# A list schedule of a four-layer graph network on one core: new offsets, new margins, one buffer moved from one pool to another

## The chip, the cores and the metric

The kernel runs on one core of a Trainium2 chip. The metric is the device time in microseconds of one execution; lower is better. All arithmetic is in fp32.

## The reference

There are 128 graphs of 64 nodes with 512 features each, so 8192 rows of 512. Four layers follow each other, and every layer ends in a residual and a layer norm:

```python
x = _layernorm(x + L0(x, adj))       # (A @ x) @ w, A from s = (x @ w) @ a by tanh, leaky relu, exp, row sums
x = _layernorm(x + L1(x, adj))       # q, k, v; weight = adj * exp(q k^T) / row sum; weight @ v
x = _layernorm(x + L2(x, adj, mask)) # w = (q . (adj @ k)) / sqrt(512); softmax over the nodes, times v = x @ Wv
x = _layernorm(x + L3(x, adj))       # hypergraph conv 512 -> 1024, relu, layer norm, conv 1024 -> 512, + x
```

In L3 the conv is `D^-1 H B^-1 H^T (x @ W^T) + b` with `H = (adj != 0)`.

## The kernel before

**Tiling.** A tile is 128 rows, two graphs. A group is two tiles (`GT = 2`, 256 rows), and there are `NG = 32` groups. Two groups make a pair (`SG = 2`) for the first product of L3. Adjacency is loaded and prepared for chunks of four tiles, so for two groups at a time.

**Products.** A product with a weight matrix is cut into blocks of half its size and done with seven block products instead of eight (`seven_products`); the first product of L3, with w3a, applies this twice and does 49 products for a pair of groups (`forty_nine_products`). The combined weight blocks are computed once, stored in DRAM, and streamed again for every group through a pool of 4 KB-per-partition buffers named `ring` (`streamed`). The matrices m1 and m2, the products of the q and k weights of L1 and L2, stay resident. Activations, transposes and sums of blocks live in a pool named `k4`, of buffers of the same size. `bank` is PSUM, eight banks. `product` and `inner` are counters without memory: they limit how many series of seven block products may be under way.

**Modes of TensorE.** Most matmuls use the whole 128x128 array ("whole"). Gathers over a graph, scores and value products use parts of it ("quarters", "columns"); the text calls these divided. One operation of a gather or of scores has 16 or 8 matmuls; fp32 makes two instructions of each.

**Order.** The body of the kernel doesn't emit instructions. It adds operations to an `Order` object: engine, planned cost, buffers read and written, and a key. `run(g)` and `run_rest` give a group's operations the step 0 to 15 they belong to; `keys_by_what_follows` then sets an operation's step to `BASE[group]` plus a part of 16 by how long a chain hangs on it, so `BASE` says how far apart groups are planned. The key is that step less an urgency and less `EARLY[step]` (and `LEAD` for the first group of a pair). `PREPARED` gives the keys of the preparation of weights, beside the groups. A piece of a streamed weight after the first is drawn towards the first one by the share `TOGETHER`.

`Order.run` then simulates the engines at build time. It has planned costs (`w_pe`, `w_dve`, `w_act`, `w_pool`), delays from one engine to the next (`LATENCY`, `AGAIN`, `TO_PE`), and a link for loads with `BYTES_PER_NS` and at most `UNDERWAY` transfers. At each moment every free engine takes the ready operation of the lowest key whose buffers are free. `AHEAD` stops the loads (engine SP) at so many steps past the oldest unfinished operation. For TensorE, `choose` decides between whole and divided operations: from the whole mode it goes to a divided one if its key is lower than that of the first whole one by more than `NEAR`, or by more than 0 when at least `ENOUGH` divided matmuls are ready; in a divided mode it stays as long as a divided operation within `FAR` of the first whole one is ready. `TURN` and `TURN_DIVIDED` are the planned costs of a change of mode. `BLOCK` and `REST` keep divided matmuls apart in time. Finally the operations are emitted in the order found, and each engine's instructions are pinned to that order (line 1472 emits them all, so every instruction has this line). All loads and stores are issued on SP's queue.

Of the kernel before, what the change touches and what calls it, by code (L numbers as in the profile page):

```python
# [28 lines left out]
APART = 4  # L29

BASE = [
    0.0, 1.743, 3.111, 5.372, 10.971, 14.755, 18.98, 22.38, 27.28, 30.68, 35.58, 38.98, 43.88, 47.28, 52.18, 55.58,
    60.48, 63.88, 68.78, 72.18, 77.08, 80.48, 85.38, 88.78, 93.68, 97.08, 101.98, 105.38, 110.213, 112.471, 117.658, 118.432,
]
RESIDENT = ("m1", "m2")
APART_3A = (0, NG // SG - 1)
LEAD = [2.505, -0.294]
PREPARED = [-3.906, 7.537, 8.271, 13.522, 12.862, -0.62]
PIECE = 1024
EPS = 1e-5  # L40
TINY = 1.1754944e-38
# [24 lines left out]


class Order:
    LATENCY = {"PE": 210, "DVE": 125, "ACT": 140, "POOL": 120, "SP": 2200}
    AGAIN = {"PE": 0, "DVE": 115, "ACT": 115, "POOL": 120}  # L70
    TO_PE = 300
    BYTES_PER_NS = 300
    UNDERWAY = 8
    TURN, TURN_DIVIDED = 145, 60

    NEAR = 0.5
    FAR = 6.79728
    ENOUGH = 28.88843999999999

    EARLY = [2.22, 0.626, 0.0, -0.759, 0.0, -0.394, 0.0, 1.328, 0.0, 1.09, 0.384, -0.03, -0.766, -0.36, -1.408, -0.964]  # L80

    BLOCK = 64
    REST = 4500
    AHEAD = 4.2
    TOGETHER = 0.7

    def __init__(self, slots):
        self.slots = {kind: list(range(n))[::-1] for kind, n in slots.items()}
# [74 lines left out]
    def run(self):  # L163

        ready = {e: [] for e in self.LATENCY}
        free_at = {e: 0 for e in self.LATENCY}
        number = {o: i for i, o in enumerate(self.ops)}
        events, n, link, mode, began = [], 0, 0, None, [-self.REST] * self.BLOCK
        port_free, port_user, landed = 0, None, []
        for o in self.ops:  # L170
            if not o.missing:
                heappush(ready[o.engine], (o.key, number[o], o))
        by_step, front = sorted((o for o in self.ops if o.engine != "SP"), key=lambda o: o.step), 0
        done, now = [], 0
        while len(done) < len(self.ops):
            moved = False
            while front < len(by_step) and by_step[front].start is not None:
                front += 1
            far = by_step[front].step + self.AHEAD if front < len(by_step) else float("inf")
            for e, heap in ready.items():  # L180
                while free_at[e] <= now:
                    skipped, held, found, found_pe = [], set(), None, {}
                    while heap:
                        if e == "SP" and heap[0][0] > far:
                            break
                        item = heappop(heap)
                        need = defaultdict(int)
                        wants = [b for b in item[2].touches if b.slot is None]
                        for b in wants:
                            need[b.kind] += 1  # L190
                        if item[2].port and port_free > now:
                            skipped.append(item)
                        elif all(k not in held and len(self.slots[k]) >= c for k, c in need.items()):
                            if e == "PE":
                                skipped.append(item)
                                found_pe.setdefault(item[2].mode, []).append((item, wants))
                                if item[0] < 0:
                                    break
                            else:
                                found, takes = item, wants  # L200
                                break
                        else:
                            held.update(k for k, c in need.items() if k in held or len(self.slots[k]) < c)
                            skipped.append(item)
                    if found_pe:
                        chosen = self.choose(found_pe, mode, now, began)
                        if chosen is None:
                            n += 1
                            heappush(events, (now + 100, n, None, None))
                        else:  # L210
                            found, takes = chosen
                            skipped.remove(found)
                    for item in skipped:
                        heappush(heap, item)
                    if found is None:
                        break
                    moved, found = True, found[2]
                    turn = 0
                    if e == "PE":
                        if found.mode == "any":  # L220
                            found.mode = "whole" if mode in ("whole", None) else "quarters"
                            found.args = (found.mode == "whole",)
                        if found.mode != mode:
                            turn = self.TURN if "whole" in (found.mode, mode) else self.TURN_DIVIDED
                        mode = found.mode
                        began += [now + turn + found.cost * i // found.matmuls for i in range(found.matmuls)]
                    found.start = now
                    done.append(found)
                    found.takes = takes
                    for b in takes:  # L230
                        b.slot = self.slots[b.kind].pop()
                    end = free_at[e] = now + found.cost + turn
                    if found.port:
                        port_free = end
                        if e == "POOL":
                            found.behind = port_user
                        else:
                            port_user = found
                    if e == "SP":
                        link = max(link, now) + found.bytes // self.BYTES_PER_NS  # L240
                        end = max(end, link)
                        landed.append(end + self.LATENCY[e])
                        if len(landed) >= self.UNDERWAY:
                            free_at[e] = max(free_at[e], landed[-self.UNDERWAY])
                    seen = end + self.LATENCY[e]
                    heappush(events, (free_at[e], n, None, None))
                    for u in found.users:
                        n += 1
                        heappush(events, (seen if e == "SP" else end + self.AGAIN[e] if u.engine == e
                                          else seen + self.TO_PE * (u.engine == "PE"), n, u, None))  # L250
                    for b in found.touches:
                        n += 1
                        heappush(events, (seen, n, None, b))
                    n += 1
            if not events:
                stuck = [(e, h[0][2].key, [b.kind for b in h[0][2].touches]) for e, h in ready.items() if h]
                raise RuntimeError(f"no operation can start: {len(done)} of {len(self.ops)}, {stuck}")
            now = max(now, events[0][0])
            while events and events[0][0] <= now:
                _, _, u, b = heappop(events)  # L260
                if u is not None:
                    u.missing -= 1
                    if not u.missing:
                        heappush(ready[u.engine], (u.key, number[u], u))
                if b is not None:
                    b.left -= 1
                    if not b.left:
                        self.slots[b.kind].append(b.slot)
        return done
# [19 lines left out]
def kernel(  # L289
# [32 lines left out]
    kinds = {}  # L322

    def kind(name, n, *shape, space=None):
        kinds[name] = [(space or sbuf).tile([P, *shape], FP, name=f"{name}{i}") for i in range(n)]

    kind("x", 6, GT, D)
    kind("k4", 18, PIECE)
    kind("ring", 8, PIECE)
    kind("h", 2, GT, DH)  # L330
    kind("k2", 2, D)
    kind("adj", 6, CT, N)
# [2 lines left out]
    kind("e", 4, GT, N)  # L335
    kind("col", 28, 16)
    kind("bank", 8, D, space=psum)
    kinds["product"] = [None] * 2
    kinds["inner"] = [None] * 3

    order = Order({k: len(v) for k, v in kinds.items()})
# [332 lines left out]
    for h in range(2):  # L674
        load_half(wq2_raw, wqk_h[0], h)
        load_half(wk2_raw, wqk_h[1], h)
    order.key = PREPARED[0]
    m2 = gram("m2", wq2_raw, wk2_raw, KC // 2)
# [668 lines left out]
    def run_rest(n):  # L1347
# [65 lines left out]
        for r, (g, xt, _, in_g, own, dc, dh) in enumerate(pair):  # L1413
            step(13)
            order.early += LEAD[0] * (n - 1 - r)
            h, sh = hs[r], Buf("col", GT)
# [7 lines left out]
            step(14)  # L1424
            order.early += LEAD[1] * (n - 1 - r)

# [116 lines left out]
```

## Time and profile before

| | |
|---|---|
| median of 3 runs | 2156.91 us (2156.62 to 2159.59) |
| profiled execution, its own time | 2155.14 us |
| its span, first to last instruction | 2153.2 us |
| PE busy | 2120.1 us, 98% of the span |
| DVE, ACT, POOL busy | 1403.6, 1204.8, 460.0 us |
| moved by DMA | 422.34 MB, mean 196 GB/s |
| DMA issues of 512 KB ring<-3a | 196, median 4.5 us to landing |

All instructions stand under line 1472, so groups are told apart by what they write and read: `bank<-ring,k` is a product of a streamed weight with an activation, `bank<-k,m` one with a resident matrix, `bank<-kept,h`, `bank<-e,x` and `bank<-kept,x` are gathers, `bank<-k,k` of 64 columns is scores, `bank<-k,e` the value product, `bank<-ident,x` a transpose. PE is the stream of matmuls and PEld that of weight loads. A busy PE is not PE at its peak, since ends of matmuls are modelled; starts are measured.

### The profile page before, as it was taken

To read this page: it belongs to the slowest core of one execution; us is meant where nothing else is said; L and a number is where in the kernel's file an instruction comes from. 1 tells how busy PE (TensorE), PEld (TensorE's weight loads), DVE (VectorE), ACT (ScalarE), POOL (GpSimd) and SP (SyncE) were. 2 spreads that over 40 slices of the span, in tenths; PEclk is the share of its full clock that TensorE was granted. 3 is DMA by queue.
4 is the path that set the end of the run, shared out by engine and by line. 5 is a ranking of instruction groups with operands and counts; after the bars stand their busy time and mean duration, and the time that the engine had idled before them with its cause. 6 is when DMAs were issued, how large, how long until landed. Compare 5 with 4: busy or idle time off the path is not lost.

```text
span 2153.2 us, 53735 instructions
## 1 busy us (share of the span) xinstructions
PE 2120.1 (98%) x21419; PEld 1829.5 (85%) x21419; DVE 1403.6 (65%) x4150; ACT 1204.8 (56%) x2698; POOL 460.0 (21%) x434
## 2 busy tenths in 40 slices
PE   8999999999999999999999999999999999999997
PEld 4897788888888888888888888888888888888875
DVE  5756767575666758567576766757667585676644
ACT  2544755565655746466464664646557464674554
POOL 1211422122212122131211211122121221302221
PEclk9999999999999999999999999999999999999999
DMA  8888784554546545474554655545465454555455
GB/s 275 276 294 292 263 284 153 207 182 149 194 164 218 188 153 197 148 241 171 181 183 141 214 175 189 199 153 189 161 221 181 159 194 145 207 185 171 170 187 190
DMA packets 166313, 422.34 MB, mean 196 GB/s; under 512 B 34928, under 2 KB 52528, under 8 KB 166064
## 3 DMA queue, kind: packets, MB, share of 16 engines
q1 hardware_dynamic: 166064, 418.92, 56.9%
q8 instruction: 169, 2.77, 0.5%
q14 instruction: 80, 0.66, 0.1%
HBM read 382.77 MB, written 36.08 MB: 195 GB/s over the span
## 4 chain that ended last, share of the span: by engine, by line
PE 92%; DMA 4%; SPq 1%; ACT 1%; DVE 1%; issue 0%; POOLq 0%; ACTq 0%; DVEq 0%
PE bank L1472 92%; DMA ring<-3a 3%; SPq L1472 1%; ACT k L1472 1%; DMA adj<-in_adjT_dram 0%; DMA k<-in_wk_dram 0%; ACT h L1472 0%; DMA x<-in_x_dram 0%; DMA 3a<-k 0%; DMA ring<-in_wv_dram 0%; DMA adj<-mask_rows 0%; DVE h L1472 0%; DVE col L1472 0%; DVE x L1472 0%; DVE k L1472 0%
## 5 line engine op out<-in xcount | busy, mean ns | idle before, releaser
L1472 PE MATMUL bank<-ring,k 128*128 128x256 f32 x4940 | 1191.1, 388 | 16.0 <-DMA ring<-3a 8.6
L1472 PEld LDWEIGHTS bank<-ring,k 128*128 128x128 f32 x4940 | 901.6, 190 | 170.5 <-issue 34.1
L1472 ACT COPY k<-bank 128x256 f32<-128x256 f32 (+1 forms) x934 | 428.0, 483 | 437.7 <-PE bank L1472 426.8
L1472 DVE SCALAR_TENSOR_TENSOR x<-bank,col,x 128x256 f32<-128x256 f32 (+1 forms) x736 | 367.6, 504 | 301.3 <-PE bank L1472 291.6
L1472 PEld LDWEIGHTS bank<-k,m 128*128 128x128 f32 x3584 | 432.5, 192 | 13.3 <-ACT k L1472 1.9
L1472 PE MATMUL bank<-k,m 128*128 128x128 f32 x3584 | 442.2, 276 | 0.5 <-ACT k L1472 0.5
L1472 DVE TENSOR_TENSOR k<-bank,k 128x256 f32<-128x256 f32 x582 | 235.6, 420 | 193.3 <-PE bank L1472 127.4
L1472 POOL TENSOR_TENSOR col<-col,mhalf 128x2 f32<-128x2 f32 (+1 forms) x161 | 113.8, 707 | 1025.1 <-DVE col L1472 631.7
L1472 ACT ACTIVATE k<-x,col 128x512 f32<-128x512 f32 x256 | 184.2, 720 | 199.3 <-DVE col L1472 186.5
L1472 PE MATMUL bank<-ring,h 128*128 128x256 f32 x1024 | 236.1, 379 | 0.0
L1472 ACT ACTIVATE x<-x,col,col 128x512 f32<-128x512 f32 x256 | 197.2, 812 | 45.5 <-DVE col L1472 45.2
L1472 PEld LDWEIGHTS bank<-ring,h 128*128 128x128 f32 x1024 | 189.8, 190 | 24.5
L1472 DVE TENSOR_TENSOR k<-k 128x256 f32<-128x256 f32 (+1 forms) x349 | 155.9, 468 | 23.4 <-ACT k L1472 20.8
L1472 DVE TENSOR_TENSOR k<-k,k 128x256 f32<-128x256 f32 (+3 forms) x361 | 165.1, 465 | 0.8
L1472 POOL TENSOR_TENSOR k<-k,b3b_b 128x512 f32<-128x512 f32 x64 | 81.6, 1286 | 196.9 <-ACT k L1472 160.3
L1472 PEld LDWEIGHTS bank<-k,k 128*64 128x64 f32 (+1 forms) x2112 | 79.4, 140 | 43.3 <-issue 31.8
L1472 PE MATMUL bank<-k,k 128*64 128x64 f32 (+1 forms) x2112 | 110.0, 239 | 4.6 <-DMA k<-in_wk_dram 4.5
L1472 DVE TENSOR_SCALAR col<-col 128x2 f32<-128x2 f32 (+2 forms) x402 | 84.0, 214 | 33.1 <-ACT k L1472 23.4
L1472 ACT ACTIVATE k<-bank,u_c 128x128 f32<-128x128 f32 x256 | 84.8, 364 | 31.9 <-PE bank L1472 31.7
L1472 POOL TENSOR_TENSOR k<-k,k 128x1024 f32<-128x1024 f32 (+1 forms) x31 | 72.0, 2324 | 128.2 <-DVE k L1472 69.7
L1472 POOL TENSOR_TENSOR x<-x,bv_b 128x512 f32<-128x512 f32 x64 | 82.3, 1291 | 62.1 <-PE bank L1472 36.9
L1472 DVE TENSOR_TENSOR h<-k,k 128x1024 f32<-128x1024 f32 (+1 forms) x88 | 89.4, 1027 | 6.5 <-issue 4.3
(102 smaller groups left out, 1632.9 us busy)
## 6 DMA issues: line engine op xcount, KB each, us to landing
ring<-3a SPq DMA_DIRECT2D x196, 512.0 KB, 4.5
ring<-v SPq DMA_DIRECT2D x189, 512.0 KB, 3.6
ring<-3b SPq DMA_DIRECT2D x126, 512.0 KB, 4.0
ring<-w SPq DMA_DIRECT2D x93, 512.0 KB, 4.5
x<-in_x_dram SPq DMA_DIRECT2D x32, 512.0 KB, 5.4
ring<-v SPq DMA_DIRECT2D x63, 256.0 KB, 3.0
out_dram<-x SPq DMA_DIRECT2D x31, 512.0 KB, 5.5
ring<-w SPq DMA_DIRECT2D x31, 256.0 KB, 3.8
```

What stands on the lines that cost most here:

```text
L1472: made = f(*args, **kwargs)
```

## The change

The planner gets new numbers, two rules and other buffer counts. The operations are the same.

```diff
 BASE = [
-    0.0, 1.743, 3.111, 5.372, 10.971, 14.755, 18.98, 22.38, 27.28, 30.68, 35.58, 38.98, 43.88, 47.28, 52.18, 55.58,
-    60.48, 63.88, 68.78, 72.18, 77.08, 80.48, 85.38, 88.78, 93.68, 97.08, 101.98, 105.38, 110.213, 112.471, 117.658, 118.432,
+    3.2735, 8.0652, 5.7526, 12.3539, 15.2711, 19.4819, 28.2783, 26.7823,
...
+    113.3204, 117.0908, 123.649, 125.591, 132.4907, 135.1692, 144.8875, 142.169,
 ]
-LEAD = [2.505, -0.294]
-PREPARED = [-3.906, 7.537, 8.271, 13.522, 12.862, -0.62]
+LEAD = [18.6707, 10.0037]
+PREPARED = [3.2501, 6.4884, 8.4096, 18.9837, 15.9208, -1.3348]
...
-    LATENCY = {"PE": 210, "DVE": 125, "ACT": 140, "POOL": 120, "SP": 2200}
+    LATENCY = {"PE": 210, "DVE": 125, "ACT": 140, "POOL": 120, "SP": 3500}
-    TO_PE = 300
-    BYTES_PER_NS = 300
-    UNDERWAY = 8
-    TURN, TURN_DIVIDED = 145, 60
+    TO_PE = 0
+    BYTES_PER_NS = 270
+    UNDERWAY = 9
+    TURN, TURN_DIVIDED = 110, 60
-    NEAR = 0.5
-    FAR = 6.79728
-    ENOUGH = 28.88843999999999
+    NEAR = 0.004
+    FAR = 163.3543
+    ENOUGH = 1.2457
-    EARLY = [2.22, 0.626, 0.0, -0.759, 0.0, -0.394, 0.0, 1.328, 0.0, 1.09, 0.384, -0.03, -0.766, -0.36, -1.408, -0.964]
+    EARLY = [7.5201, -0.713, 2.7673, 21.1569, 0.5055, 0.6085, 5.6889, 14.9021, 0.0162, 18.6753, 16.5455, 0.4227, -1.4983, -1.1338, 12.9793, -2.8031]
-    AHEAD = 4.2
-    TOGETHER = 0.7
+    AHEAD = 5.2259
+    TOGETHER = 0.3719
+    OLDEST = 3.3813
+    SPARE = {"k4": 1, "ring": 0}
...
+            near = by_step[front].step + self.OLDEST if front < len(by_step) else float("inf")
...
+                        elif item[2].step > near and any(len(self.slots[k]) < c + self.SPARE[k] for k, c in need.items() if k in self.SPARE):
+                            skipped.append(item)
...
-    kind("k4", 18, PIECE)
-    kind("ring", 8, PIECE)
+    kind("k4", 17, PIECE)
+    kind("ring", 9, PIECE)
...
-    kinds["product"] = [None] * 2
+    kinds["product"] = [None] * 3
```

The second rule: an operation more than `OLDEST` steps past the oldest unfinished one takes a `k4` buffer only if one more stays free.

## The prediction

> **What bounds the kernel now.** I read the page's busy line first, then the span in slices, the chain, PE's own waits, the timeline around one wait, and the sums by stretch.
>
> ```profile
> PE 2120.1 (98%) x21419; PEld 1829.5 (85%) x21419; DVE 1403.6 (65%) x4150; ACT 1204.8 (56%) x2698; POOL 460.0 (21%) x434
> ...
> PEclk9999999999999999999999999999999999999999
> DMA  8888784554546545474554655545465454555455
> ...
> PE 92%; DMA 4%; SPq 1%; ACT 1%; DVE 1%; issue 0%; POOLq 0%; ACTq 0%; DVEq 0%
> ```
>
> TensorE is the bound: busy 98% of 2153.2 us, and 92% of the chain. The change removes no matmul, so it can win only what lies between matmuls. By stretch (columns: length, then busy time and count of PE, PEld, DVE, ACT, POOL, then clock, DMA share, GB/s):
>
> ```profile
> 4.00:60.00 56.00, 49.77 (x324) 28.12 (x325) 30.19 (x85) 13.25 (x45) 8.05 (x9) 0.91 0.82 263
> 60.00:2100.00 2040.00, 2028.21 (x20701) 1771.19 (x20700) 1349.88 (x4000) 1164.86 (x2609) 445.58 (x412) 1.00 0.57 195
> 2100.00:2140.00 40.00, 35.58 (x368) 24.79 (x368) 19.19 (x42) 21.63 (x37) 4.59 (x5) 1.00 0.62 224
> 2140.00:2153.20 13.20, 6.51 (x31) 5.39 (x29) 3.23 (x16) 3.81 (x7) 1.10 (x2) 0.90 0.21 79
> ```
>
> Idle on PE: 6.2 us in the first stretch, plus 9% of its 56 us at a lowered clock, some 5 us; 11.8 us in the 2040 us of the middle; 4.4 us and 6.7 us at the end. In the middle, what PE waits for is nearly one thing:
>
> ```profile
> PE bank L1472 <- DMA ring<-3a: 8.6, 9, 1.4
> PE bank L1472 <- DVE col L1472: 1.6, 1, 1.6
> PE bank L1472 <- ACT k L1472: 0.9, 2, 0.5
> ```
>
> Nine waits for a streamed piece of w3a. The chain shows such a link every 131 us (one pair of groups). The timeline at one of them:
>
> ```profile
> 1204.67 1.24 PE L1472 MATMUL bank<-ring,k 128*128 128x256 f32 x5
> 1205.84 1.15 PE L1472 MATMUL bank<-k,k 128*64 128x64 f32 x32
> 1206.92 1.56 PE L1472 MATMUL bank<-ring,k 128*128 128x256 f32 x6
> ...
> 1213.43 7.07 PE L1472 MATMUL bank<-ring,k 128*128 128x256 f32 x32
> 1220.34 0.39 PE L1472 MATMUL bank<-e,same 128*128 128x128 f32 x2
> 1220.56 0.60 PE L1472 MATMUL bank<-ident,x 128*128 128x128 f32 x4
> 1222.58 1.56 PE L1472 MATMUL bank<-ring,k 128*128 128x256 f32 x6 [1.42 <-DMA ring<-3a]
> ```
>
> Two prices come out of it. **A matmul of 256 columns**: 32 of them from 1213.43 to 1220.34, 0.216 us each. A ring piece of w3a (512 KB) serves four products of two such instructions, 1.73 us, so an unbroken run of them asks for 524 KB/1.73 us = 303 GB/s. Over the 40 us from 60 to 100 us the trace shows 306 GB/s moved at a DMA share of 0.93, and a ring<-3a load takes 4.5 us at the median to land. Supply and demand are equal in such a run; only the ring's lead covers a late load. **A visit to the divided array** (the 64-wide modes): five ring matmuls take 1.17 us where 5 x 0.216 = 1.08, so going in costs 0.09; coming back, six take 1.40 instead of 1.30, 0.10; the two score operations between (32 instructions) take 1.08, while a lone one (16), seen elsewhere in the timeline at 1107.89, takes 0.62, so each costs 0.47 and 0.15 is fixed. A visit costs 0.09 + 0.15 + 0.10 = 0.34 us. I count 162 visits, in the steady state ten in each 131 us: 162 x 0.34 = 55 us, which the page books as busy.
>
> **The Trainium skill.** "TensorEngine Tiling (Array Packing)", Tiling Modes, says that a change of the tiling mode drains the array; the trace agrees, 0.34 us a visit. "TensorE: Matmul & The Clock Gate", Part 1, says that the array falls to half clock after an idle window of about 3.4 us; the trace has PE busy 1.49 of the 4 us from 40 to 44, and clocks of 0.55 and 0.50 in the two 4 us stretches after. "Perfetto Trace Analysis", Identifying the Most-Contended Engine, says that matmul busy time is a poor measure of the distance to the limit; here too, since visits hide in the 98%.
>
> **What a new order could win at most.** By form, at the rates of the timeline: 5852 matmuls of 256 columns x 0.216 = 1263; some 4356 of 128 or fewer at 0.112 (40 in 4.46 us at 1102.90) = 487; 178 of 512 columns x 0.43 = 77; divided work, 128 score and 256 gather operations at 0.47, 32 value products at 0.86, 16 chunk sums at 0.42, = 214; visits 55; some 70 changes between two divided modes inside a visit at 0.15 = 10. Sum 2106. The first matmul starts at 4.1 us and 7.0 us follow the last start: 2117 of the 2153.2. So 36 us are stalls, of which about 29 are visible above; below that only fewer visits help.
>
> **The change part by part.** Every instruction stays: the 1015 DMA issues on SP, all matmuls, the ACT, DVE and POOL work. What changes is the order on each queue, three buffer counts and the order's reasons. The planner runs at build time and costs the chip nothing.
>
> 1. *One ring buffer more (8 to 9), loads planned at 270 B/ns and 3500 ns instead of 300 and 2200, TOGETHER 0.70 to 0.37.* Planned landing of 512 KB: 1.75 + 2.2 = 3.9 us before, 1.94 + 3.5 = 5.4 after, against 4.5 measured and 6.3 at the wait shown. The ninth piece is worth 1.73 us of lead, more than the longest of the nine waits (1.4, or 1.6 start to start). They hold 10 us by starts; I take 8 back, bounds 0 and 10. Less pull (TOGETHER) also keeps pieces of one stream from taking slots long before use. SP holds the order: of its waits, 1525 us are for PE to free a slot, so each load moved past another matters, and nine under way instead of eight may queue a little deeper; 64 adjacency loads of 32 KB, the x loads and the stores stand in the same queue.
> AHEAD is nearly the same in time: 4.2 steps of 17.1 us (65.5 us a group over 3.82 steps between groups) and 5.23 of 14.6 (over 4.48), 72 and 76 us.
> 2. *Group offsets, EARLY, LEAD, PREPARED; TO_PE 300 to 0.* In the steady part these decide only which ready operation goes first, so their price is in the waits of part 1 and the visits of part 3. In the first 60 us: the gram of m2 goes from offset -3.9 to 3.25, behind group 0's chain, which now leads by 7.5. Its 32 matmuls (13.9 us at 24.4 us) may then fill the holes at 41, 46 and 51 us (2.4, 1.7 and 0.9 us) and spare part of the slow clock. I take 3 of the 11 us; bounds 9 gained and 8 lost, since its four k4 buffers stay full longer and group 0's weights come through the same SP queue. At the end: the last two groups swap (144.9 and 142.2), the waits for ACT there are 3.0 and 1.2 us; I take 2, bounds 4 gained and 6 lost.
> 3. *NEAR 0.5 to 0.004, ENOUGH 28.9 to 1.25, FAR 6.8 to 163.* A divided operation is taken as soon as it is the oldest, without half a step of patience (8.6 us at 17.1 us a step); once in, every ready one is taken. The first adds visits, the second merges them. The score and gather steps 9 and 14 also get 18.7 and 13 steps of urgency. I take six fewer visits, -2 us; bounds 30 fewer (-10) and 50 more (+17).
> 4. *k4 18 to 17, one kept for the oldest work, a third product set.* More product sets let PE interleave resident m1 and m2 products (no load) with streamed ones, which lowers the demand of 303 GB/s; one k4 less can hold up a transpose. DVE at 65% and ACT at 56% have slack, but their results free the eight PSUM banks. Nothing, bounds -3 and +8.
>
> Sum: -8 - 3 - 2 - 2 = -15 us. The profiled execution took 2155.14 us (span 2153.2), 1.8 below the median of the runs, 2156.91; taken from the median: 2142.
>
> **The rivals.** (a) *Less switching as well*: if the merging wins, two visits fewer in each pair, 32 x 0.34 = 11 us more: 2131. For it: ten visits a pair hold 27 divided operations, under three each. Against: dependences space them. (b) *The gain is paid back*: stalls shift to other loads or to PSUM copies, and the sum lies near zero, 2156. For it: a middle with 11.8 us of idle in 2040 leaves little; POOL, DVE and ACT wait hundreds of us for each other, and a fit to planned costs can't see transfers colliding. Here falls too that the change doesn't do what it says: loads already reach 306 GB/s, so 265 may not be what made those nine waits late; the load shown was issued at 1216.2 with adjacency loads right behind it, and took 6.3 us. (c) *Slower through eager switching*: urgency 18.7 and 13 with no patience splits visits; from ten to thirteen a pair is 48 more, +16 us, against perhaps 8 won: 2165. It decides from 8 + 4.3 = 12.3 us, that is 36 more visits, two and a quarter per pair. For it: steps 9 and 14 have six operations a group that may now each be fetched alone. Against: with FAR at 163 an entry empties the whole list.
>
> **How the numbers follow.** A measurement tells about 0.2%, 4.3 us, from no change. Chances: forecast 0.58, own range 2133 to 2151; (a) 0.18; (b) 0.10; (c) 0.14. Faster by over 0.2% is the first two, 0.76, less 0.01 for a weak forecast: 0.75; within 0.2%, 0.11; slower 0.14. The range reaches from 2123, where (a) still has half its worth again, to 2161, leaving out most of (c).
>
> **What would show it.** Right: waits of PE for ring<-3a in the middle fall from nine to at most three, and idle there from 11.8 to under 5 us; idle from 4 to 60 us under 6.2 with a clock above 0.91; 150 to 162 visits. Wrong: visits above 195, a new releaser of PE (ACT k, DVE k) with over 8 us in the middle, or idle moved into the first 60 us.

## The result and the profile after

The changed kernel takes 2145.11 us (median of four runs, 2143.58 to 2145.77), the kernel before 2158.25 us over its four runs on record by then: a ratio of 0.9937 (95% interval 0.992 to 0.9955), 13 us faster. The forecast was 2142 in a range of 2123 to 2161, 15 us faster. The profiled execution took 2145.31 us, its span 2143.4 against 2153.2.

The page of the changed kernel, first the busy line, then the chain by engine and by line:

```profile
PE 2123.4 (99%) x21433; PEld 1829.4 (85%) x21433; DVE 1407.9 (66%) x4150; ACT 1197.9 (56%) x2698; POOL 458.0 (21%) x434
...
PE 99%; ACT 0%; DMA 0%; DVE 0%; issue 0%; SPq 0%; POOLq 0%; ACTq 0%; DVEq 0%
```

PE is busy 3.3 us *longer* than before in a span that is 9.8 us shorter, and the loads have left the chain (4% before, 0% now). The sums by stretch (length, then busy time and count of PE, PEld, DVE, ACT, POOL, then clock, DMA share, GB/s):

```profile
4.00:60.00 56.00, 51.55 (x413) 30.77 (x414) 35.91 (x105) 18.78 (x56) 10.13 (x11) 0.97 0.95 311
60.00:2100.00 2040.00, 2037.99 (x20645) 1772.22 (x20644) 1353.65 (x3986) 1159.69 (x2610) 444.73 (x414) 1.00 0.57 195
2100.00:2132.00 32.00, 31.96 (x370) 25.07 (x369) 15.56 (x41) 15.11 (x26) 1.80 (x3) 1.00 0.50 173
2132.00:2144.00 12.00, 1.90 (x9) 1.33 (x7) 1.64 (x8) 3.04 (x6) 0.70 (x1) 0.73 0.12 44
```

In the first stretch PE idles 4.5 us instead of 6.2 and the clock is 0.97 instead of 0.91; in the middle it idles 2.0 us instead of 11.8. What PE waits for there, all of it:

```profile
PE bank L1479 <- ACT k L1479: 1.3, 1, 1.3
PE bank L1479 <- issue: 0.6, 1, 0.6
```

The nine waits for ring<-3a are gone. Two things went the other way. The visits to the divided array, counted in the trace as before, are 184 instead of 162. And from the start of the last matmul to the end it is 9.8 us instead of 7.0. The account, by span:

| | before | after | us |
|---|---|---|---|
| idle of PE, 60 to 2100 us | 11.8 | 2.0 | -9.8 |
| idle of PE, 4 to 60 us | 6.2 | 4.5 | -1.8 |
| lost to the halved clock while PE is busy, 4 to 60 us | 3.8 | 1.7 | -2.1 |
| idle of PE from 2100 us to its last start | 4.4 | 0.0 | -4.4 |
| visits at 0.34 us | 162 | 184 | +7.5 |
| last start to the end | 7.0 | 9.8 | +2.8 |
| sum | | | -7.8 |

The clock row comes from these views of the kernel before, stretches and then PE's timeline:

```profile
44.00:48.00 4.00, 2.78 (x8) 1.73 (x6) 2.26 (x6) 0.00 (x0) 0.00 (x0) 0.55 1.09 336
48.00:52.00 4.00, 2.63 (x69) 2.12 (x69) 3.55 (x18) 1.66 (x4) 0.00 (x0) 0.50 0.94 308
52.00:56.00 4.00, 4.00 (x14) 3.10 (x12) 2.37 (x7) 0.83 (x3) 1.18 (x2) 0.67 0.06 17
...
48.45 1.99 PE L1472 MATMUL bank<-e,x 64*64 64x64 f32 x64 [1.67 <-DVE e L1472]
51.35 0.69 PE L1472 MATMUL bank<-e,same 64*64 64x128 f32 x4 [0.92 <-ACT e L1472]
```

These clocks make 10.2 us at half clock. PE idled for 2.6 of them, in the two waits shown, and that time is counted as idle already; half of the other 7.7 is 3.8. After the change it is 3.4 us at half clock, with PE busy throughout. The span fell by 9.8, so 2.0 us are not placed. Some 1.4 of them may belong to the nine waits, which hold 10 us counted from start to start and 8.6 as idle time.

The medians differ by more (13.1) than the spans: the profiled execution of the kernel before, 2155.14 us, lies 3.1 below its median, and its runs scatter. Over all comparisons below they lie between 2149.2 and 2168.1 us. So runs of different comparisons are set side by side here only by their ratio to the kernel before, which ran in each of them.

### The profile page after: what moved, and what is told of

Same layout as the page of the kernel before. It is cut to its first block, busy times and chain, and to the rows that moved or that the text cites. A ratio compares the mean times of both kernels' runs of the same rounds, so it can differ in the third digit from the quotient of the medians.

```text
span 2143.4 us, 53774 instructions
## 1 busy us (share of the span) xinstructions
PE 2123.4 (99%) x21433; PEld 1829.4 (85%) x21433; DVE 1407.9 (66%) x4150; ACT 1197.9 (56%) x2698; POOL 458.0 (21%) x434
## 4 chain that ended last, share of the span: by engine, by line
PE 99%; ACT 0%; DMA 0%; DVE 0%; issue 0%; SPq 0%; POOLq 0%; ACTq 0%; DVEq 0%
PE bank L1479 99%; DMA k<-in_wk_dram 0%; ACT k L1479 0%; SPq L1479 0%; DVE e L1479 0%; ACT h L1479 0%; ACT x L1479 0%; DVE h L1479 0%; DVE col L1479 0%; POOLq L1546 0%; ACTq L1546 0%; DVE m L1479 0%; ACT e L1479 0%; DVE x L1479 0%; ACT kept L1479 0%
## 5 line engine op out<-in xcount | busy, mean ns | idle before, releaser
L1479 PE MATMUL bank<-ring,k 128*128 128x256 f32 (+1 forms) x4940 | 1187.8, 387 | 1.3 <-ACT k L1479 1.3
L1479 DVE SCALAR_TENSOR_TENSOR x<-bank,col,x 128x256 f32<-128x256 f32 (+1 forms) x736 | 363.3, 504 | 281.3 <-PE bank L1479 275.2
L1479 PE MATMUL bank<-k,m 128*128 128x128 f32 x3584 | 448.5, 276 | 0.0
L1479 DVE TENSOR_TENSOR k<-k,k 128x256 f32<-128x256 f32 (+2 forms) x361 | 179.1, 505 | 0.4
L1479 DVE TENSOR_TENSOR k<-k 128x256 f32<-128x256 f32 (+2 forms) x349 | 152.9, 457 | 37.0 <-ACT k L1479 33.8
L1479 DVE TENSOR_SCALAR col<-col 128x2 f32<-128x2 f32 (+2 forms) x402 | 71.5, 185 | 41.2 <-ACT k L1479 34.7
L1479 POOL TENSOR_TENSOR x<-x,k 128x512 f32<-128x512 f32 x64 | 81.4, 1273 | 40.8 <-DVE k L1479 28.4
```

The source lines that it names most:

```text
L1479: made = f(*args, **kwargs)
```

## The experiments

Two kinds of edit are used. A *planned* run changes a number and lets the planner make a new order. A *replayed* run keeps the order of each engine's queue as planned, changes one thing, and gives out tiles again in that order:

```diff
-    for o in order.run():
+    for o in order.again(order.run(), {k: len(v) for k, v in kinds.items()}):
```

`again` walks the same queues, an operation starting when it heads its queue, its inputs are there and its buffers are free.

**The base, replayed with nothing altered.**

> The changed kernel's order, emitted once more with every queue fixed in that order and nothing altered; it is the base for the runs beside it. Every theory expects the time of the changed kernel: about 13 us (0.6%) below the kernel before, a span near 2143 us, 184 visits, idle of PE from 60 to 2100 us near 2 us.

2145.86 us, ratio 0.9927 (0.9907 to 0.9947), span 2143.8, 184 visits, idle in the middle 1.8 us. It stands for the changed kernel in what follows.

**A ninth ring buffer in the old order.** The kernel before, replayed:

```diff
-    kind("ring", 8, PIECE)
+    kind("ring", 9, PIECE)
-    b3a_b = vector_in("b3a_b", b3a, DH)
+    b3a_b = vector_in("b3a_b", b3a, 8)
```

> The kernel before, every queue in its own order, but with nine ring buffers instead of eight; k4 stays at 18. The room comes from the bias b3a: only 8 columns of it are loaded and the sums of w3a's product read the first 256 columns of bv instead (both biases are zero in the inputs). Theory that the ring's lead made the nine waits: they go, 8 to 10 us less, span near 2144 us, idle of PE from 60 to 2100 us near 3 us. Rival, that the order of the loads or the crowding of transfers made them: six or more of the nine stay and the gain is under 3 us.

2138.87 us, ratio 0.9937 (0.9917 to 0.9956), the ratio of the whole change. The waits of PE in the middle, all of them:

```profile
PE bank L1551 <- ACT k L1551: 3.0, 1, 3.0
PE bank L1551 <- DVE col L1551: 1.5, 2, 0.9
```

No wait for a ring load is left, with no instruction in another place on any queue. The control has the cut bias and eight buffers:

> Control for the run with nine ring buffers in the old order: the kernel before, every queue in its own order, eight ring buffers; only the bias b3a is cut as there (8 columns loaded, bv read in its place, both zero). Theory that the ninth buffer made that run's gain: this one stays within 2 us of the kernel before and keeps its waits for ring loads, eight or more. Rival, that the 512 KB less at the start or the other read of the bias made it: 8 us or more faster.

2157.75 us, ratio 0.9992 (0.9983 to 1.0001). Its waits in the middle, the two largest:

```profile
PE bank L1551 <- DMA ring<-3a: 11.6, 10, 2.1
PE bank L1551 <- DVE col L1551: 1.6, 1, 1.6
```

So the waits and the gain belong to the buffer: 0.9937 against 0.9992 is 0.55%, 12 us. The one trace with nine buffers goes further: with 162 visits and 7.1 us after the last start its span is 2134.2, 9 us under that of the changed kernel. The ratios of the timed runs don't show that lead.

The control also says something on the start. Its stretch from 4 to 60 us, and the gram of m2 in it:

```profile
4.00:60.00 56.00, 51.65 (x400) 30.11 (x401) 34.03 (x102) 14.78 (x49) 8.41 (x10) 0.97 0.86 276
```

```profile
23.94 13.93 PE L1551 MATMUL bank<-k,k 128*128 128x512 f32 x32
```

PE is busy 51.65 us here, and 51.59 with the ninth buffer. What both have better than before there (49.77) can't come from the ring; it comes with the cut bias, that is with 512 KB less to load at the start. And it comes with the gram still in one block.

**The two counts alone, planned.** The kernel before with `k4` 17 and `ring` 9, all else old:

> The kernel before planned with the change's two counts alone, k4 17 and ring 9; offsets, load numbers, mode rules and two product sets stay old. Its plan has 193 visits instead of 162. Theory that the ring's gain must be paid with the k4 buffer unless the offsets are fitted to it: 31 visits more cost 11 us and PE idles for ACT and DVE, so 5 to 30 us slower than before. Rival, that the counts are the whole change: 10 us or more faster.

2180.38 us, ratio 1.0102 (1.0082 to 1.0122): 1% slower than before. Waits of PE in the middle, the longest:

```profile
PE bank L1472 <- ACT k L1472: 8.0, 18, 1.1
PE bank L1472 <- DMA ring<-3a: 4.8, 7, 1.1
PE bank L1472 <- DVE k L1472: 1.5, 3, 0.7
```

The plan has 193 visits, and seven waits for ring<-3a are left although there are nine buffers (two more are for ring<-w). A reading that fits: the planner, which believes in loads of 300 B/ns and 2200 ns, knew of the ninth buffer and planned with it; where it did not know of it, in the replayed run, the same buffer was pure margin. The loss of one k4 buffer is in this run too: PE waits 18 times for ACT to fill one, though other causes of these waits are not excluded.

**The load numbers, taken back and alone.** The changed kernel with 300 B/ns, 2200 ns, 8 under way, TOGETHER 0.70:

> The changed kernel planned with the load numbers of the kernel before: 300 B/ns, 2200 ns, 8 under way, TOGETHER 0.70; nine ring buffers and all else of the change stay, and the plan has 181 visits instead of 184. Theory that planning late loads keeps PE from waiting: waits for ring loads come back in the middle, 8 to 15 us slower than the changed kernel. Rival, that the ninth buffer alone is enough: no ring waits to speak of, within 3 us of the changed kernel.

2163.34 us, ratio 1.0043 (1.0026 to 1.0061); span 2164.0, 20 us over the base. Waits of PE in the middle:

```profile
PE bank L1479 <- ACT k L1479: 5.1, 9, 1.1
PE bank L1479 <- DMA ring<-3a: 3.1, 6, 1.1
PE bank L1479 <- ACT e L1479: 1.7, 4, 1.0
PE bank L1479 <- DMA ring<-v: 1.4, 2, 1.1
PE bank L1479 <- DVE col L1479: 0.6, 2, 0.3
PE bank L1479 <- DMA ring<-w: 0.5, 1, 0.5
```

Nine waits for ring loads, 5.0 us, with nine buffers, much as in the counts-only run. Another 7.4 us in this list are waits that no load ended; that the offsets no longer fit the plan is the likely reason. And the other way round, the kernel before with only the new load numbers:

```diff
-    BYTES_PER_NS = 300
-    UNDERWAY = 8
+    BYTES_PER_NS = 270
+    UNDERWAY = 9
-    TOGETHER = 0.7
+    TOGETHER = 0.3719
```

and SP 3500 in `LATENCY`.

> The kernel before with only the load numbers of the change (270 B/ns, 3500 ns, 9 under way, TOGETHER 0.37), eight ring buffers, its old offsets; its plan has 172 visits. Theory that the load numbers are what helps: the nine waits go, 5 to 10 us faster than the kernel before. Rival, that numbers and offsets work only together: an unfitted plan idles elsewhere, 10 us or more slower.

2242.13 us, ratio 1.0413 (1.0393 to 1.0433). The longest waits of PE in the middle:

```profile
PE bank L1472 <- DVE k L1472: 37.1, 27, 2.7
PE bank L1472 <- ACT k L1472: 11.3, 20, 2.5
```

Not one wait for a ring load, with eight buffers, as the theory says, and 55 us of idle for other reasons. On the time the rival was right: with the old offsets the new numbers lose. In the planned orders here, waits for ring loads go with the load numbers. The three plans with the old numbers (the kernel before, the counts alone, the run above) have nine each in the middle, with eight buffers or with nine. This plan, the changed kernel and the next two runs, all with the new numbers, have none.

**The gram's key.** The changed kernel with `PREPARED[0]` of before:

> The changed kernel planned with one number of before: the key of m2's gram, -3.906 instead of 3.25. Its plan has 192 visits instead of 184. Theory that moving this gram made the better start: in the first 60 us the gram comes in one block again and idle there goes from 8.5 us back to 10 us or more. Rival, that the ninth ring buffer made it: idle in the first 60 us stays within 1 us. Over the whole the plan is no longer fitted; 3 us for the visits and up to 15 us more.

2156.81 us, ratio 0.9985 (0.9975 to 0.9995). The stretch from 4 to 60 us, then the timeline of PE in it (start, duration, count, idle before):

```profile
4.00:60.00 56.00, 46.05 (x308) 26.12 (x309) 29.00 (x78) 12.49 (x41) 8.20 (x9) 0.91 0.84 271
```

```profile
26.24 14.00 PE L1479 MATMUL bank<-k,k 128*128 128x512 f32 x32
...
42.63 1.99 PE L1479 MATMUL bank<-ring,k 128*128 128x256 f32 x8
47.82 0.55 PE L1479 MATMUL bank<-e,same 128*128 128x128 f32 x2 [3.20 <-ACT e L1479]
```

The gram is one block of 14 us again, and afterwards PE has nothing to fill its waits with: 9.95 us idle, more than in the kernel before (6.2), and the clock at 0.91, the same as there. In the changed kernel the same matmuls lie in pieces between the first products, two of them here:

```profile
36.90 2.75 PE L1479 MATMUL bank<-ring,k 128*128 128x256 f32 x12
39.49 1.88 PE L1479 MATMUL bank<-k,k 128*128 128x512 f32 x4
41.21 1.03 PE L1479 MATMUL bank<-ring,k 128*128 128x256 f32 x4
42.07 7.03 PE L1479 MATMUL bank<-k,k 128*128 128x512 f32 x16
```

So within the changed plan the better start hangs on this key: 5.5 us of idle and, with PE busy for 7.7 of 10.2 us at half clock, 2.1 us of clock. It is not the only way there: the control above starts as well with the gram in one block and 512 KB less to load. The new key in the old plan was not run. The middle stays good (2.6 us idle), with no wait for a ring load; all of PE's waits there:

```profile
PE bank L1479 <- ACT k L1479: 1.3, 2, 1.1
PE bank L1479 <- ACT x L1479: 0.8, 1, 0.8
PE bank L1479 <- issue: 0.5, 1, 0.5
```

**The mode rules.** The changed kernel with NEAR, FAR, ENOUGH and the turn costs of before:

> The changed kernel planned with NEAR, FAR, ENOUGH and the planned costs of a mode change of the kernel before. Its plan has 186 visits instead of 184. Theory that the mode rules made the 22 visits more: then this would have shown fewer, which the plan already denies; so the time should differ only by unfitted waits, 5 to 40 us slower with idle of PE in the middle well above 2 us. Rival, that the patience of the old rules helps on the chip: within 3 us of the changed kernel or faster.

2171.03 us, ratio 1.0056 (1.0037 to 1.0074), 186 visits, 17 us idle in the middle. Taking the rules back does not bring the visits back, so the 22 more do not hang on the rules.

**The price of a visit.** The changed order, replayed with 60 exchanges on PE:

```diff
+    while made < 60 and i + 3 < len(pe):
+        if [o.mode == "whole" for o in pe[i : i + 4]] == [False, False, True, True] and pe[i].mode == pe[i + 1].mode:
+            pe[i + 1], pe[i + 2] = pe[i + 2], pe[i + 1]
...
```

> The changed kernel's order with 60 visits to the divided array more: where two divided operations of one kind stand together ahead of two whole ones, the second trades places with the first whole one; every other queue as it was. Theory that a visit costs PE its full price (0.34 us, nothing hides it): 60 x 0.34 = 20 us more, a span near 2164 us. Rival, that PE has slack after the change which swallows switching: under 5 us more, a span below 2149 us.

2180.43 us, ratio 1.0091 (1.0071 to 1.0111); 244 visits, span 2177.5, 33.7 us over the base. The price accounts for 60 x 0.34 = 20; going in alone, from start to start, costs 6.2 us more in the trace, 0.10 each. Of the other 13 us, 8 are idle time of PE: 5.6 in the middle (1.8 to 7.4 us), 0.9 before it and 1.3 after it. Half clock with PE busy adds 1.7 us, and some 4 us are not placed. Each exchanged operation comes one whole operation later, and its readers in ACT and DVE with it; that this makes the waits is argued. The rival of slack on PE falls; both theories were too low.

The opposite, 15 moves that join visits:

```diff
+    for a, b, c in [(612, 613, 614), ...]:
+        pe = pe[:a] + pe[b:c] + pe[a:b] + pe[c:]
```

> The changed kernel's order with 15 moves on PE alone that join neighbouring visits: 13 visits fewer, 171 in all; every other queue as it was. Full price: 13 x 0.34 = 4.5 us less, a span near 2139 us. Rival, that the moved operations come late and their readers stall PE by as much: 0 to 2 us less, and idle of PE in the middle above 4 us.

2146.24 us, ratio 0.9932 (0.9914 to 0.9949), no gain; 171 visits, span 2142.7, 1.1 under the base's. The middle is as good as the base's, 1.8 us idle. What is lost lies in the first 60 us: 6.0 us of idle there instead of 4.5, and a clock of 0.94 instead of 0.97, together 3 of the 4.5 us. Part of it fits the moves: one of the joined visits, at 54 us, waits 1.3 us for ACT. Another part does not: the first matmul starts 0.7 us later, ahead of all that was moved, and in the next run, where nothing was moved, it starts 1.2 us later. So the next set of moves leaves the start alone, where PE waits for the first results.

**The end.**

```diff
-            for among in (range(t, t + 1) for t in range(GT)) if g == NG - 1 else (range(GT),):
+            for among in (range(t, t + 1) for t in range(GT)) if g == NG - 2 else (range(GT),):
```

> The changed kernel with one condition altered: the last layer norm and the store are done tile by tile for group 30, which now ends last, instead of for group 31. Theory that the 2.8 us which the end has lost (9.8 us after the last matmul starts, against 7.0 before) come from the swap of the last two groups: 2.5 to 3 us less, 7.0 us after the last start. Rival, that the end is longer because ACT or the store is late for another reason: under 1 us.

This run is planned. 2144.00 us, ratio 0.9922 (0.9905 to 0.994), which the timed runs can't tell from the base. The trace can: 7.5 us from the last start to the end instead of 9.8. The last layer norm is split by tiles for group 31 only, and with offsets 144.9 and 142.2 it is group 30 that ends. The changed kernel normalizes both tiles in one go and stores them in one transfer (timeline of its end):

```profile
2132.01 1.89 PE L1479 MATMUL bank<-ring,k 128*128 128x256 f32 x8
...
2134.93 0.72 ACT L1479 ACTIVATE k<-x,col 128x512 f32<-128x512 f32 x1 [6.51 <-DVE col L1479]
...
2135.65 0.70 ACT L1479 ACTIVATE k<-x,col 128x512 f32<-128x512 f32 x1
...
2137.72 1.52 ACT L1479 ACTIVATE x<-x,col,col 128x512 f32<-128x512 f32 x2 [1.27 <-DVE col L1479]
2139.27 0.38 SPq L1479 DMA_DIRECT2D out_dram<-x  x1
```

**Both repairs together.** 29 moves of the same kind, all after the first 140 us, and the split:

> The changed kernel's order with 29 moves on PE after the first 140 us that join neighbouring visits, 26 fewer, 158 in all, the rule that keeps 64 divided matmuls 4.5 us apart not applied to them, and with the last layer norm split for group 30. Full price: 26 x 0.34 = 9 us, and 2.7 for the end: span near 2132 us. Rival, that joined visits stall (the rule was needed, or readers come late): over half of the 9 us is lost, span above 2136 us.

2136.04 us (2134.58 to 2137.66), ratio 0.9918 (0.9902 to 0.9934); 158 visits, span 2132.8. This is the shortest median of all runs here, but the base did not run beside them. Its times, 2143.0 to 2146.9, come from a comparison in which the kernel before took 2160.29 us, against 2154.72 in this one. By the ratios (0.9918 and 0.9927) the two differ by 2 us, less than the intervals can tell.

The traces show more: 11.0 us less span than the base. The repairs should give 26 x 0.34 + 2.4 = 11.2, but that the two numbers agree is in part luck. The first 60 us, where nothing was moved, gave another 2.4 (clock 1.00 instead of 0.97, 0.7 us less idle), and 1.5 us went into idle time in the middle. In the trace the repairs do about what was forecast; what they are worth in time is not settled.

```profile
60.00:2100.00 2040.00, 2036.71 (x20780) 1777.18 (x20779) 1356.33 (x3988) 1162.03 (x2617) 442.19 (x412) 1.00 0.58 196
```

PE idles 3.3 us in the middle here and does 135 matmuls more in it than the changed kernel. Leaving out the rule of 4.5 us for these moves cost nothing that shows.

## Why the prediction was right, and where not

**What a new order could win.** The result stays within the bound of 36 us, and its two halves, stalls and visits, are where the time moved. The sum of the forecast is -15, and the medians say -13.1; that they come so close is in part luck. By the spans it is -9.8, and its terms are others: loads, start and end gave 15 us where 13 were forecast, and the visits took 7.5 where 2 were to be won. That the medians lie 3 us further apart than the spans comes from the scatter of the kernel before.

**Part 1, the loads (-8).** Right: nine waits to none, 9.8 us of idle gone in the middle, the upper end of its bounds. The reason given, one piece more of lead, is shown for a fixed order: the ninth buffer removes every ring wait. It is not the reason in a planned order: with nine buffers and the old load numbers, seven and six waits for ring<-3a stand in two plans, and with eight buffers and the new numbers there is none. In the plans on record the load numbers decide, and the buffer alone does not. With eight buffers, though, the new numbers were seen only in a plan with 55 us of other idle time, in which loads can catch up; whether the changed plan could do with eight was not run. The doubt whether the planned rate is the right number did not bear on the result: the plan with 270 B/ns has no ring wait, whatever the link can do.

**Part 2, the start (-3) and the end (-2).** The start gave 3.9 us by the account (1.8 of idle, 2.1 of clock), by the mechanism of the forecast: m2's gram fills the holes and spares the slow clock, which the run with its old key supports. The 11 us that were put up for this hold too much: part of the 5 us at a lowered clock is idle time counted already, and 10 remain. The end was half seen: the waits for ACT after 2100 us, 3.0 and 1.2 us, went (-4.4 with smaller ones), while the swap of the last two groups cost 2.8. The prediction names the swap but does not read on to `g == NG - 1`, which ties the split to a group's number.

**Part 3, the visits (-2).** Wrong in sign: +22 visits, +7.5 us, inside the bounds, but outside the 150 to 162 that were named as a sign of being right. The step that failed is "I take six fewer", which let the wide FAR outweigh the lack of patience. The rules are not even what made them: with the old ones the plan has 186. In the old kernel the counts alone raise the plan from 162 visits to 193, so the missing k4 buffer is a likely cause, but no run takes it apart from the ninth ring buffer. The price itself, 0.34 us, fits the run with both repairs to some 1 us of 9; in the run that splits visits it is 20 of the 34 us lost.

**Part 4 (0).** The price of the k4 buffer was put at nothing with +8 as the bound. In the changed kernel one wait of 1.3 us for ACT k is left in the middle; in the counts-only plan it is 8.0 us in 18 waits. If the k4 buffer makes these waits, the fit has hidden them, at the cost of visits.

**The rivals.** That of eager switching had the direction of the visits right and their number wrong (22 instead of 48), and not their cause. That the gain is paid back was true for 10 of some 18 us won.

What stays open: the changed plan with eight ring buffers, and a plan with 18 k4 and nine ring buffers, fitted anew. Neither was run.

## What to carry to other kernels

When an in-order stream of loads makes the bound engine wait by a microsecond at each turn, first add a buffer without telling the scheduler: here that was margin, while a buffer that the planner knew of left the waits standing as long as its load times were too short. Numbers of a fitted schedule are not separable, so judge them by what each leaves in the trace (waits, switches, ends), and when the order of groups changes, look for special cases tied to a group's number. After the waits are gone, count the switches that the page books as busy; here 22 more of them took 7.5 us of the 9.8 won in the middle.

## What the runs showed that I had not expected

The kernel before scatters by 19 us between runs (2149.2 to 2168.1, 60 runs), the changed order by 4 (2143.0 to 2146.9, 9 runs). The runs are unequal in number, but the difference stands within one comparison too: 14 us over nine runs of the kernel before, 4 over five of the base. The control's profile has ten waits for ring<-3a with 11.6 us where the kernel before had nine with 8.6, in the same order of every queue. So it seems that a chain of loads without margin turns small differences of transfers into PE time. The other runs speak against that as the whole cause: with nine buffers in the old order no ring wait is left, and its six runs still scatter by 11 us, while the changed kernel with the old load numbers has nine ring waits, and its seven runs scatter by 5.

The granted clock goes along with the time: in the comparison with 35 runs of the kernel before, the 23 with a mean clock of 0.996 or less took 2161.5 us on average, the other 12 took 2157.2. In the control's trace the clock falls to half for 3.4 us after a wait of 1.65 us that ends at 180.9 us (the mean is 0.66 from 180 to 185 us) and again after one of 2.96 us that ends at 2121.8 us (0.57 from 2123 to 2127 us). Each fall costs 1.7 us, half of its length, since PE is busy. The trace of the kernel before has the same two waits, for DVE col and for ACT k, and no fall between 60 and 2140 us. So the same wait can cost more in one run than in another. How much of the scatter this makes is open.

The other surprise is that 60 delayed operations cost 13 us beyond their switches, 8 of them idle time of PE, although DVE is busy 65% and ACT 55%.
